# Node sums by three small products, pair 1's marks behind the first layer, and a quad's weights in one iteration

## The chip, the cores and the metric

The kernel runs on one core of one Trainium2 chip. A core has a matrix engine (TensorE, called PE in the profile, with its weight loads shown apart as PEld), a vector engine (VectorE, DVE), a scalar engine (ScalarE, ACT), a general engine (GpSimd, POOL) and a sequencer that issues most DMAs (SyncE, SP). They run side by side, each through its own instructions in the order in which these were written, and wait for each other through semaphores. The metric is the device time of one execution in microseconds (us), over several runs. The profiled execution has a time of its own and a span, from its first to its last instruction.

## The reference, cut to what matters

A graph layer over 128 graphs of 64 nodes with 128 features. Every pair of nodes (i, j) gets a message from a three-layer perceptron; the messages are masked by the adjacency `adj[b, i, j]` (0 or 1, about an eighth of it set, the diagonal always) and summed over j; a second perceptron updates the node.

```python
pair_feats = concat([f_i, f_j], axis=-1)
h = layernorm(relu(pair_feats @ w0 + b0))
h = layernorm(relu(h @ w1 + b1))
messages = (h @ w2 + b2) * adj[..., None]
agg = sum(messages, axis=2)
out = x + mlp_upd(concat([x, agg], axis=-1))
```

Messages where `adj` is 0 count for nothing, so only the edges that are set need computing. The layer norms have gain one and shift zero here, but the kernel takes them as they come.

## The kernel before, in words

**Edges as slots.** Each graph gets 640 slots, one per edge, packed in order of node; the slots are five tiles of 128. Two graphs make a *pair* (64 of them, both graphs side by side on the 128 partitions), two pairs a *quad* (32), four pairs a *block* (16). Slots are worked on in *chunks* of 512 columns: five chunks a quad, ten a block, 160 in all. A flag at the end of the kernel sends graphs with more than 640 edges, or weights other than 0 and 1, through a second, dense path; with these inputs it isn't taken.

**Finding the slots of a block.** `rank` (DVE, L354) makes running sums of the adjacency along each row, so its last column is each node's degree. `count` (PE, L363) multiplies the degrees by the triangular matrix `lt` (one triangle for each graph of a pair): that gives the sums of degrees up to and with each node, `cumall`. `count_out` and `degrees` copy both to SBUF on ACT. `place` (POOL, L374) takes the degrees off `cumall` (`before`: the sum of the nodes ahead), adds the two (`mid`: twice the middle of the node's range of slots), and adds `before` to the ranks (`pos`). `place_out` masks `pos` by the adjacency into `posall`, and `odd_marks` and `odd_weights` prepare the check for weights other than 0 and 1.

**Gather lists of a pair.** A slot belongs to a node if its distance from `mid` is less than the degree: `distance` (ACT, L467) and `make_tp` (DVE, L473) make `tp`, a 0/1 matrix of nodes by slots. `node_rows` (ACT, L479) casts it, and `stack` (SP, L486) copies it by DMA into the upper half of `S[p]`. `marks` (PE, L495) multiplies `posall` by `tp`, and `compare` (DVE, L503) compares the outcome with the slot's number, which gives a 0/1 matrix of the second nodes; another `stack` puts it into the lower half of `S[p]`. Pair 0 is done ahead of the loop, without DMA: its compares write `S[0]` at once. Pair 1 has its marks, compares and stacks ahead of the loop too.

**The chunk pipeline.** `layer0` (PE, L521) multiplies the projected features of both nodes (`abl` and `abh`, a low and a high part, made from `xnT` by `rows`, `rows_hi` and `rows_lo`) by the slots of `S`, and ACT evicts it with relu as `h`. `stats0` turns `h` on PE (L530) and DVE takes its statistics. Eight iterations later `layer1` (PE: a bias product at L567, then L570) goes into the one bank `z`, ACT evicts it as `y` (L573), and `stats1` takes its statistics. At a quad's end `var0_of` (POOL, L247 to L251) makes `m`, `root_of` takes the root on ACT (`m_sd`), casts its high part on ACT (`sh`, L548) and makes the low part on POOL (`sh`, L549), and `turn_root` (PE, L554) turns it for the bias product. `var1_step`, `root1_of` and `inverse_of` give the second norm's factors `m_q`. `node_marks` turns `tp` by a DMA into `oh`, `weights` (POOL, L636; DVE for the last quad) multiplies `oh` by the factors for each of the two graphs of a pair, and `reduce` (PE, L651) sums `y` by node.

**Updates.** Each block has a `Unit` (the last block two) that runs the second perceptron: `sums_out`, `turn`, `layer` (PE, L696 and L710), `layer_out` (DVE), the roots with POOL's `um_v` and ACT's `um_sq`, the biases `m0` and the residual `xo` on POOL, and `finish`.

**The order of the work.** It is written out by hand. `at(n, place, fn)` puts a step into iteration `n` of the main loop at a named place; the loop runs the places in the order a, m, layer 1, b, layer 0, stats0, k, stats1, x, x1, x2, e0, e1, e. So each engine's queue is the order in which these steps are called. `L1` is 8 iterations, a quad has `QC` = 5. The steps for the turned root of a quad q stand in iteration 5q + 6; before the change the weights of quad q's even pair stand in iteration 5q + 15 and those of its odd pair in 5q + 16, in place e1. Behind the weights come the residual and the bias of a unit, then `place` of a later block, all in place e. Buffers that matter: one PSUM bank each for `mk`, `hps`, `hT` and `z`; four `S`; two each of `d`, `i`, `j` and `w`.

**The start.** Loads are issued on SP in the order in which they are first used, the first layer's two weight matrices on ACT. Seven products of a constant run on PE while they land. `place_first` (DVE, L395) makes `before` and `mid` of block 0, and `place_pair` (DVE, L407) the masked positions of one pair of it.

Of the kernel before, what the change touches and what calls it, by code (L numbers as in the profile page):

```python
# [23 lines left out]
def tile_gnn(  # L24
# [68 lines left out]
    def mat(ap, name, eng=nc.sync):  # L93
        return load(ap, [P, C], name, eng)
# [11 lines left out]
    def load_first(b, q0, q1):  # L106
        nc.sync.dma_start(xn0[:, b, q0:q1], xf[(b * PB + q0) * P:(b * PB + q1) * P, :]
                          .rearrange("(q p) c -> p q c", p=P))

    nc.sync.dma_start(an0[:, 0], adjp[:, 0:PB, :])  # L110
    load_first(0, 0, 2)
    w0a = mat(mw0[0:C, :], "w0a", nc.scalar)
    w0b = mat(mw0[C:2 * C, :], "w0b", nc.scalar)
# [29 lines left out]
    lt = const.tile([P, P], F32, name="lt")  # L143
    nc.gpsimd.memset(lt, 1.0)
    nc.gpsimd.affine_select(out=lt, in_=lt, pattern=[[1, P]], compare_op=ALU.is_ge,
                            fill=0.0, base=0, channel_multiplier=-1)
    nc.gpsimd.memset(lt[0:N, N:P], 0.0)
# [4 lines left out]
    make_identity(nc, ident)  # L152

# [12 lines left out]
    cumall = const.tile([P, NP], F32, name="cumall")  # L166
# [120 lines left out]
    def edge_path(es):  # L287
# [72 lines left out]
        def count(b):  # L360
            blk = blocks[b]
            blk["ps"] = abank()
            nc.tensor.matmul(blk["ps"][:, 0:PB], lhsT=lt, rhs=blk["rk"][:, :, N - 1], start=True,  # L363
                             stop=True)

        def count_out(b):
            nc.scalar.copy(cumall[:, b * PB:(b + 1) * PB], blocks[b].pop("ps")[:, 0:PB])
# [6 lines left out]
        def place(b):  # L374

            blk = blocks[b]
            cum = cumall[:, b * PB:(b + 1) * PB]
            before = adp.tile([P, PB], F32, name="before")
            nc.gpsimd.tensor_tensor(before, cum, blk["deg"], op=ALU.subtract)
            blk["mid"] = adp.tile([P, PB], F32, name="mid")  # L380
            nc.gpsimd.tensor_tensor(blk["mid"], cum, before, op=ALU.add)  # L381
            pos = adp.tile([P, PB, N], F32, name="pos")
            nc.gpsimd.tensor_tensor(pos, blk.pop("rk"),
                                    before.unsqueeze(2).to_broadcast([P, PB, N]), op=ALU.add)
            blk["pos"] = pos
# [9 lines left out]
        def place_first():  # L395
            blk = blocks[0]
            rk = blk["rk"]
            before = blk["before"] = adp.tile([P, PB], F32, name="before")
            nc.vector.tensor_tensor(before, cumall[:, 0:PB], rk[:, :, N - 1], op=ALU.subtract)
            blk["mid"] = adp.tile([P, PB], F32, name="mid")  # L400
            nc.vector.tensor_tensor(blk["mid"], cumall[:, 0:PB], before, op=ALU.add)

        def place_pair(q):
            blk = blocks[0]
            for g in range(2):
                s = slice(g * N, (g + 1) * N)
                nc.vector.scalar_tensor_tensor(posall[s, 0, q, g, :], blk["rk"][s, q],  # L407
                                               blk["before"][s, q:q + 1], blk["an"][s, q],
                                               op0=ALU.add, op1=ALU.mult)
# [54 lines left out]
        def distance(p):  # L464
            b, q = divmod(p, PB)
            D[p] = tpp.tile([P, CAP], F16, name="d", bufs=2)
            nc.scalar.activation(D[p], slot, AF.Abs, bias=blocks[b]["mid"][:, q:q + 1], scale=-1.0)  # L467
# [347 lines left out]
        for p in range(NP):  # L815
            n = p * TG * 2 // CH
            if p > 1:
                at(max(n - 7, p - 2), "a", distance, p)
                at(max(n - 6, p - 2), "m", make_tp, p)
                at(max(n - 5, 1), "a", node_rows, p)  # L820
                at(max(n - 4, 1), "a", stack, p, 0, IR)
                for k in range(2):
                    at(n - 5 + k, "k", marks, p, k)
                    at(n - 5 + k, "k", compare, p, k)
                at(n - 3, "a", stack, p, 1, JR)
            w = p // 2 * QC + QC + L1 + p % 2
            last = p // 2 == NQ - 1
            at(w - 4, "a", node_marks, p)
            at(NCHK + L1 + 1 if last else w + 2, "e1", weights, p)
            at(NCHK + L1 + 2 if last else p // 2 * QC + SC, "x1", reduce, p)  # L830
# [19 lines left out]
        rank(0)  # L850
        count(0)
        count_out(0)
        turn_x(0, 0, 2)
        turn_x_out(0, 0, 2)
        degrees(0)
        place_first()
# [4 lines left out]
        rows_hi(0, 0)  # L861
# [4 lines left out]
        for g in range(2):  # L866
            s = slice(g * N, (g + 1) * N)
            nc.scalar.copy(S[0][0:N, g, :], TP[0][s])
# [4 lines left out]
            if g == 0:  # L873
                rows_lo(0, 0)
                distance(1)
        MK.pop((0, 0)), MK.pop((0, 1))
        place_pair(1)
        make_tp(1)
        node_rows(1)
        stack(1, 0, IR)  # L880
        for k in range(2):
            marks(1, k)
            compare(1, k)
        stack(1, 1, JR)
        nc.vector.memset(ones_row, 1.0)
        at(0, "x", turn_x, 0, 2, PB)
        at(0, "a", lambda: place_pair(2))
        at(1, "m", lambda: place_pair(3))
        at(1, "a", lambda: turn_x_out_rest())
        at(1, "e", odd_marks, 0)  # L890
# [230 lines left out]
```

## Time and profile before

| | us |
|---|---|
| median of three runs | 614.89 (614.76 to 615.21) |
| the profiled execution | 615.34 |
| its span | 613.6 |
| PE busy | 577.3 |
| DVE busy | 478.1 |
| ACT busy | 379.1 |
| POOL busy | 361.7 |
| one block of the steady part, start to start | 35.04 |

A line of the timeline has the start and the duration in us, the engine and line, the operation with the tiles that it writes and reads, the shape, the number of instructions that are merged in it, and in brackets how long the engine had been idle and what ended that. PE's ends are modelled, so distances between starts are the safer figures. A line of the list of waits has who waited for whom, the total in us, how many times, and the longest. One PE product in full precision shows as two passes (x2), a transpose as one.

### The profile page before, as it was taken

Reading aid. Unit: us, or ns where it says so; the run is one execution under the profiler, and the core shown is the slowest. Engines: PE = TensorE matmul, PEld = TensorE weight load, DVE = VectorE, ACT = ScalarE, POOL = GpSimd, SP = SyncE. Lnnn points to the kernel's source line nnn. Section 1 sums busy time; section 2 is a strip of 40 time slices with the busy share of each in tenths; the row PEclk is TensorE's granted clock in tenths of the full one; section 3 lists DMA queues with packets and bytes.
Section 4 is the critical chain, followed back from the end, with each engine's and each line's share of the span. In section 5 each row is a group of like instructions: output and inputs, shape, how many; then the busy total and the mean of one; then the engine's idle time right before and its main releaser. Section 6 shows DMA issues by size and latency. Waiting matters only on the chain. (4 is left out here: it accounts for less than half of the span.)

```text
span 613.6 us, 15457 instructions
## 1 busy us (share of the span) xinstructions
PE 577.3 (94%) x5393; PEld 532.1 (87%) x5393; DVE 478.1 (78%) x1868; ACT 379.1 (62%) x781; POOL 361.7 (59%) x919
## 2 busy tenths in 40 slices
PE   5888999999999999999999999999999999998875
PEld 4677889998999999898999999899999989898763
DVE  5767668897878889787878889787888978776574
ACT  4676666676667567576656667666656657653412
POOL 2634375675838476574839567583847657463742
PEclk9999999999999999999999999999999999999987
DMA  4654455545354663734464554535544444331101
GB/s 100 155 126 116 105 114 115 93 118 114 86 144 117 121 116 103 117 89 118 118 132 107 130 96 114 117 85 142 118 121 106 108 114 97 86 84 41 24 18 37
DMA packets 91085, 63.84 MB, mean 104 GB/s; under 512 B 57462, under 2 KB 74876, under 8 KB 91004
## 3 DMA queue, kind: packets, MB, share of 16 engines
q1 hardware_dynamic: 90716, 62.69, 45.1%
q8 instruction: 44, 0.72, 0.5%
q14 instruction: 37, 0.30, 0.2%
q10 hardware_dynamic: 288, 0.13, 0.1%
HBM read 6.82 MB, written 4.19 MB: 18 GB/s over the span
## 5 line engine op out<-in xcount | busy, mean ns | idle before, releaser
L534 DVE BATCH_NORM_STATS2 st<-hT 128x6 f32<-128x128 f32 x640 | 141.9, 284 | 49.0 <-PE hT L530 47.3
L570 PEld LDWEIGHTS z<-w1c,h 128*128 128x128 f32 x1280 | 168.3, 192 | 6.9
L570 PE MATMUL z<-w1c,h 128*128 128x128 f32 x1280 | 168.8, 275 | 0.0
L580 DVE BATCH_NORM_STATS2 st<-y 128x6 f32<-128x128 f32 x640 | 137.7, 277 | 14.7 <-ACT y L573 14.6
L573 ACT ACTIVATE y<-z 128x512 f32<-128x512 f32 x160 | 95.2, 595 | 77.4 <-PE z L570 77.4
L524 ACT ACTIVATE h<-hps,b0c 128x512 f32<-128x512 f32 x160 | 109.3, 683 | 2.3 <-PE hps L521 2.2
L247 POOL TENSOR_TENSOR m_d<-st 128x20 f32<-128x20 f32 x62 | 15.5, 250 | 146.7 <-DVE st L534 131.1
L530 PE MATMUL hT<-ident,h 128*128 128x128 f32 x640 | 97.2, 275 | 0.0
L636 POOL TENSOR_TENSOR w<-oh,m_q 128x320 f32<-128x320 f16 x124 | 91.8, 761 | 5.8 <-PE hT L530 5.0
L521 PE MATMUL hps<-s,abl 128*128 128x512 f32 (+3 forms) x256 | 92.1, 372 | 0.4 <-ACT h L524 0.4
L530 PEld LDWEIGHTS hT<-ident,h 128*128 128x128 f32 x640 | 76.3, 141 | 9.9 <-DVE st L534 0.3
L567 PE MATMUL z<-b1t,sdT 80*128 80x512 f32 x160 | 78.4, 490 | 1.6 <-ACT y L573 1.6
L521 PE MATMUL hps<-s,abh 128*128 128x512 f32 (+3 forms) x256 | 78.3, 324 | 0.0
L651 PE MATMUL ys<-y,w 128*64 128x128 f32 x1280 | 77.1, 275 | 0.0
L651 PEld LDWEIGHTS ys<-y,w 128*64 128x64 f32 x1280 | 69.3, 137 | 7.3 <-issue 7.0
L467 ACT ACTIVATE d<-slot,mid 128x640 f16<-128x640 f16 x64 | 53.3, 833 | 34.2 <-POOL mid L381 34.2
L503 DVE TENSOR_TENSOR j<-mk,cmpt 128x320 fp32r<-128x320 f32 x126 | 59.6, 473 | 1.6 <-PE mk L495 1.6
L458 DVE TENSOR_TENSOR abl<-mu,abh 128x512 fp32r<-128x512 f32 x32 | 22.1, 691 | 39.9 <-ACT abh L451 39.9
L521 PEld LDWEIGHTS hps<-s,abl 128*128 128x128 f32 x256 | 49.5, 193 | 1.8 <-ACT i L479 0.9
L479 ACT CAST i<-tp 128x640 fp32r<-128x640 f16 x63 | 45.5, 722 | 7.5 <-DVE tp L473 7.4
L521 PEld LDWEIGHTS hps<-s,abh 128*128 128x128 f32 x256 | 49.5, 193 | 0.0
L451 ACT CAST abh<-mu 128x512 fp32r<-128x512 f32 x32 | 18.8, 587 | 45.8 <-PE mu L444 45.8
(221 smaller groups left out, 1017.3 us busy)
## 6 DMA issues: line engine op xcount, KB each, us to landing
s<-i SPq DMA_DIRECT2D x126, 160.0 KB, 2.7
s<-j SPq DMA_DIRECT2D x126, 160.0 KB, 2.6
xn<-in_x_dram SPq DMA_DIRECT2D x15, 256.0 KB, 3.9
out_dram<-uo SPq DMA_DIRECT2D x15, 256.0 KB, 2.4
an<-in_adj_dram SPq DMA_DIRECT2D x16, 128.0 KB, 2.7
oh<-tp SPq DMA_TRANSPOSE x64, 2.7
xn<-in_x_dram SPq DMA_DIRECT2D x2, 128.0 KB
out_dram<-uo SPq DMA_DIRECT2D x2, 128.0 KB
```

The costliest lines, as they stand in the source:

```text
L467: nc.scalar.activation(D[p], slot, AF.Abs, bias=blocks[b]["mid"][:, q:q + 1], scale=-1.0)
L503: nc.vector.tensor_tensor(JR[p][:, c], MK.pop((p, k))[:, 0:HC], cmpt[:, c], op=ALU.is_equal)
L521: nc.tensor.matmul(ps[:, c:c + w], lhsT=ab[:, g % 4, :], rhs=s, start=(k == 0), stop=(k == 1))
L524: nc.scalar.activation(H[n], ps, AF.Relu, bias=b0c)
L530: nc.tensor.transpose(ps[:, t, :], H[n][:, t * P:(t + 1) * P], ident)
L534: nc.vector.bn_stats(ST0[q][:, CH * c + t, :], ps[:, t, :])
L567: nc.tensor.matmul(ps, lhsT=SD[q], rhs=W["b1t"][:, CH * c:CH * c + CH, :], start=True, stop=False, skip_group_check=True)
L570: nc.tensor.matmul(ps[:, t, :], lhsT=h[:, t * P:(t + 1) * P], rhs=W["w1c"], start=False, stop=True, skip_group_check=True)
L573: nc.scalar.activation(Y[n], ps, AF.Relu)
L580: nc.vector.bn_stats(ST1[q][:, CH * c + t, :], Y[n][:, t, :])
L636: (nc.vector if p // 2 == NQ - 1 else nc.gpsimd).tensor_tensor(w[:, :, g, :], OH[p][:, :, g * N:(g + 1) * N], Q[q][:, k:k + TG].unsqueeze( ...
L651: nc.tensor.matmul(YS[b][g * N:(g + 1) * N, k, :], lhsT=w[:, t, g, :], rhs=y, start=(t == 0), stop=(t == TG - 1))
```

## The change

Four edits to the order of the work, and one to how the sums are made.

1. *Sums.* `lt` becomes three matrices: the triangle, the triangle without its diagonal, and their sum. `count` multiplies the degrees by all three, so that PE gives `cumall`, `before` (as `befall`) and `mid` (as `midall`), and `count_out` copies all three at once. `place` keeps only `pos`; `place_first` is gone; `distance` reads `midall`, so it waits for ACT's own copy only.
2. *Loads.* The first two pairs' features are loaded through ACT's queue, the first layer's two weight matrices through SP's.
3. *The first block.* The features are turned ahead of the count. Pair 0's node rows come ahead of `rows_hi`, pair 1's place and `tp` ahead of the second graph's compares. Pair 1's marks, compares, node rows and stacks move into iteration 0 of the loop, behind layer 0 of chunk 0. `place_pair` of pairs 2 and 3, `odd_marks(0)` move to later places.
4. *Pairs 2 and 3.* `distance` and `make_tp` a step later or the same, marks and compares and the second stack one iteration later, the first stack at p + 1.
5. *Weights.* Both pairs of a quad have their weights in iteration 5q + 16, behind `sh` of the quad that is turned there.

```diff
-    load_first(0, 0, 2)
-    w0a = mat(mw0[0:C, :], "w0a", nc.scalar)
-    w0b = mat(mw0[C:2 * C, :], "w0b", nc.scalar)
+    load_first(0, 0, 2, nc.scalar)
+    w0a = mat(mw0[0:C, :], "w0a")
+    w0b = mat(mw0[C:2 * C, :], "w0b")
...
+    nc.gpsimd.tensor_tensor(lt[:, 1], lt[:, 0], ident, op=ALU.subtract)
+    nc.gpsimd.tensor_tensor(lt[:, 2], lt[:, 0], lt[:, 1], op=ALU.add)
...
-    cumall = const.tile([P, NP], F32, name="cumall")
+    cums = const.tile([P, 3, NP], F32, name="cums")
+    cumall, befall, midall = (cums[:, k] for k in range(3))
...
-            nc.tensor.matmul(blk["ps"][:, 0:PB], lhsT=lt, rhs=blk["rk"][:, :, N - 1], start=True,
-                             stop=True)
+            for k in range(3):
+                nc.tensor.matmul(blk["ps"][:, k * PB:(k + 1) * PB], lhsT=lt[:, k],
+                                 rhs=blk["rk"][:, :, N - 1], start=True, stop=True)
...
-            nc.scalar.copy(cumall[:, b * PB:(b + 1) * PB], blocks[b].pop("ps")[:, 0:PB])
+            nc.scalar.copy(cums[:, :, b * PB:(b + 1) * PB],
+                           blocks[b].pop("ps")[:, 0:3 * PB].rearrange("p (k q) -> p k q", k=3))
...
-            cum = cumall[:, b * PB:(b + 1) * PB]
-            before = adp.tile([P, PB], F32, name="before")
-            nc.gpsimd.tensor_tensor(before, cum, blk["deg"], op=ALU.subtract)
-            blk["mid"] = adp.tile([P, PB], F32, name="mid")
-            nc.gpsimd.tensor_tensor(blk["mid"], cum, before, op=ALU.add)
             pos = adp.tile([P, PB, N], F32, name="pos")
             nc.gpsimd.tensor_tensor(pos, blk.pop("rk"),
-                                    before.unsqueeze(2).to_broadcast([P, PB, N]), op=ALU.add)
+                                    befall[:, b * PB:(b + 1) * PB].unsqueeze(2).to_broadcast([P, PB, N]),
+                                    op=ALU.add)
...
-            nc.scalar.activation(D[p], slot, AF.Abs, bias=blocks[b]["mid"][:, q:q + 1], scale=-1.0)
+            nc.scalar.activation(D[p], slot, AF.Abs, bias=midall[:, p:p + 1], scale=-1.0)
...
-                at(max(n - 7, p - 2), "a", distance, p)
-                at(max(n - 6, p - 2), "m", make_tp, p)
-                at(max(n - 5, 1), "a", node_rows, p)
-                at(max(n - 4, 1), "a", stack, p, 0, IR)
+                early = p < PB
+                at(p - 1 if early else n - 7, "a", distance, p)
+                at(p - 1 if early else n - 6, "m", make_tp, p)
+                at(p if early else n - 5, "a", node_rows, p)
+                at(p + 1 if early else n - 4, "a", stack, p, 0, IR)
                 for k in range(2):
-                    at(n - 5 + k, "k", marks, p, k)
-                    at(n - 5 + k, "k", compare, p, k)
-                at(n - 3, "a", stack, p, 1, JR)
+                    at(n - 5 + early + k, "k", marks, p, k)
+                    at(n - 5 + early + k, "k", compare, p, k)
+                at(n - 3 + early, "a", stack, p, 1, JR)
...
-            at(NCHK + L1 + 1 if last else w + 2, "e1", weights, p)
+            at(NCHK + L1 + 1 if last else p // 2 * QC + QC + L1 + 3, "e1", weights, p)
...
+        turn_x(0, 0, 2)
         count(0)
+        degrees(0)
+        turn_x_out(0, 0, 2)
         count_out(0)
-        turn_x(0, 0, 2)
-        turn_x_out(0, 0, 2)
-        degrees(0)
-        place_first()
         distance(0)
         place_pair(0)
         make_tp(0)
         rows(0, 0)
-        rows_hi(0, 0)
...
+        node_first(0)
+        rows_hi(0, 0)
+        compare_first(0)
+        rows_lo(0, 0)
+        distance(1)
+        node_first(1)
         place_pair(1)
         make_tp(1)
-        node_rows(1)
-        stack(1, 0, IR)
+        compare_first(1)
+        MK.pop((0, 0)), MK.pop((0, 1))
         for k in range(2):
-            marks(1, k)
-            compare(1, k)
-        stack(1, 1, JR)
+            at(0, "k", marks, 1, k)
+            at(0, "k", compare, 1, k)
+        at(0, "b", node_rows, 1)
+        at(0, "e", stack, 1, 0, IR)
+        at(0, "e", stack, 1, 1, JR)
         nc.vector.memset(ones_row, 1.0)
         at(0, "x", turn_x, 0, 2, PB)
-        at(0, "a", lambda: place_pair(2))
-        at(1, "m", lambda: place_pair(3))
+        at(0, "e", place_pair, 2)
+        at(1, "e", place_pair, 3)
         at(1, "a", lambda: turn_x_out_rest())
-        at(1, "e", odd_marks, 0)
+        at(6, "e", odd_marks, 0)
```

`node_first(g)` and `compare_first(g)` are the node rows and the two compares of pair 0's graph g, as they stood in the loop before.

## The prediction, made before the changed kernel was run

> **What bounds the kernel now.** I began with the page's busy shares and its 40 slices: TensorE (PE) is busy for 94% of the span and at "9" from slice 5 to slice 37, so the kernel is bound by PE's order of work, except in the first 30 us and the last 50 us.
>
> ```profile
> PE 577.3 (94%) x5393; PEld 532.1 (87%) x5393; DVE 478.1 (78%) x1868; ACT 379.1 (62%) x781; POOL 361.7 (59%) x919
> ...
> PE   5888999999999999999999999999999999998875
> ```
>
> Next the list of who waits for whom, for PE's few waits. The largest is on `sh`, the last step of a quad's standard deviations on GpSimd (POOL); the second is in the first block. ScalarE (ACT) waits a lot for `mid`, but ACT isn't the bound.
>
> ```profile
> PE ma L554 <- POOL sh L549: 10.6, 18, 1.9
> ...
> PE mk L495 <- DVE tp L473: 4.6, 2, 3.4
> ...
> ACT d L467 <- POOL mid L381: 34.2, 13, 2.7
> ```
>
> Then the timeline of one steady block (two quads, 35.04 us start to start, the same for twelve blocks). PE's lines around the node count and around the two turned roots (L554):
>
> ```profile
> 303.19 0.60 PE L696 MATMUL ma<-ident,ysum 128*128 128x128 f32 x4
> 303.54 0.48 PE L567 MATMUL z<-b1t,sdT 80*128 80x512 f32 x1
> ...
> 307.69 0.27 PE L554 MATMUL ma<-ident,sh 128*80 128x128 f32 x1
> ...
> 310.86 0.60 PE L428 MATMUL ma<-ident,xn 128*128 128x128 f32 x4
> 311.30 0.28 PE L363 MATMUL ma<-rk,lt 128*128 128x4 f32 x2
> 311.44 0.48 PE L567 MATMUL z<-b1t,sdT 80*128 80x512 f32 x1
> ...
> 324.14 1.05 PE L710 MATMUL mu<-u1c,uhT 128*128 128x128 f32 x8
> 325.57 0.31 PE L554 MATMUL ma<-ident,sh 128*80 128x128 f32 x1 [0.38 <-POOL sh L549]
> ```
>
> One root of a block comes without a wait, the other waits. POOL shows why: two weight products stand between `m` and `sh`, although ACT's half of `sh` was cast by 324.53.
>
> ```profile
> 323.52 0.41 POOL L251 TENSOR_TENSOR m<-m_d,m_s 128x20 f32<-128x20 f32 x1
> 323.89 1.40 POOL L636 TENSOR_TENSOR w<-oh,m_q 128x320 f32<-128x320 f16 x2
> 325.25 0.27 POOL L549 TENSOR_TENSOR sh<-m_sd,sh 128x40 fp32r<-128x40 f32 x1
> 325.48 1.40 POOL L636 TENSOR_TENSOR w<-oh,m_q 128x320 f32<-128x320 f16 x2
> 326.83 1.29 POOL L690 TENSOR_TENSOR xo<-xn,cu2b 128x512 f32<-128x512 f32 x1
> ```
>
> [...] weight loads around L363 start 0.11 us apart, for 4 moving columns as for 128. [...] passes are 0.21 us apart until 19.6 us and 0.11 after it. [...]
>
> **The change, part by part.** All times are of the profiled execution (span 613.6, 615.34 us in all).
>
> *1. Three count products in place of one.* One is two passes with 128 weight columns. With it the four transposes at 310.86 lead to L567 after 0.58 us; without it the same four (303.19) lead to L567 after 0.35. So one product costs 0.23, two more about 0.45 us per block. PE has no wait from there to 325.57, and that wait is on POOL's work on statistics that come after the count on PE, so nothing absorbs it. Blocks 2 to 15 pay it at full clock: 14 x 0.45 = **+6.3**. (Blocks 0 and 1 are in part 5.) ACT's copy of 12 columns instead of 4 stays 0.17 us, in ACT's free time.
>
> *2. Weights after `sh`.* In a steady block POOL then waits for ACT's cast (324.53), runs `sh` at 324.61 to 324.88 (the 0.08 us from cast to `sh` as at 45.60/45.68), and PE can turn at 324.93. PE itself is free at 325.03 (L710's eight passes, 0.11 each), against 325.57: -0.54. But POOL now idles from 323.93 to 324.61, so its four weights end later: `xo` starts at 324.61 + 0.225 + 4 x 0.68 = 327.56 instead of 326.83, +0.73. Removing `before` and `mid` (330.44 to 330.87) gives back 0.43, so `um_v` comes 0.29 later. ACT waits for `um_v`, and `y`, which frees PE's bank, stands behind it:
>
> ```profile
> 333.16 0.30 ACT L271 ACTIVATE um_sq<-um_v,eps_c 128x4 f32<-128x4 f32 x1 [0.32 <-POOL um_v L265]
> 333.37 0.57 ACT L677 COPY ysum<-ys 128x512 f32<-128x512 f32 x1
> 333.83 0.59 ACT L451 CAST abh<-mu 128x512 fp32r<-128x512 f32 x1
> 334.87 0.60 ACT L573 ACTIVATE y<-z 128x512 f32<-128x512 f32 x1 [0.44 <-PE z L570]
> ```
>
> ACT could take `y` 0.5 us after `abh` starts, at 334.33; it will be 334.62. PE's `z`, moved 0.54 ahead, is ready for it at 334.33. So `y` is 0.29 late, and PE's next L567, which today follows `y` by 0.05 us, loses that. Behind `abh` on DVE, `abl`, `tp` and the statistics move by the same 0.29 and hold the next transposes another 0.08. Left: -0.54 + 0.29 + 0.08 = -0.17, for twelve blocks (115.32 to 500.77): **-2.0**. At 535.59 no later block is placed, which spares POOL a further 0.6 us (`pos`): the gain stays, **-0.5**. Of the early roots, 81.61 gains 0.63 (81.61 to 80.98; no update unit's roots yet in that block); 63.66 would gain 0.63, but `cu2b_b`'s copy ends at 63.40 and holds the next product: 0.37. Together **-1.0**. 31.81 and 46.00 have no weights before them: 0. Reduction stands two iterations behind the weights and keeps over 1 us. In the block's other quad POOL waits 2.06 us for DVE after the weights, which covers the later end.
>
> *3. The end.* For quad 29 POOL runs the first weights at 566.75, in idle time. Afterwards all four stand behind `sh` (569.56), so `xo`, `m` and `um_v` are 2 x 0.68 later, and ACT already waits for `um_v` with `ysum` and `y` queued behind:
>
> ```profile
> 576.46 0.30 ACT L271 ACTIVATE um_sq<-um_v,eps_c 128x4 f32<-128x4 f32 x1 [2.43 <-POOL um_v L265]
> ...
> 577.78 0.51 PE L567 MATMUL z<-b1t,sdT 80*128 80x512 f32 x1 [0.72 <-ACT y L573]
> ```
>
> PE's wait at 577.78 grows by the whole of it, and what follows is a chain: **+1.4**.
>
> *4. Sums without POOL and DVE.* ACT's `d` no longer waits for `mid` (34.2 us in all). In these stretches PE is reducing and never waits for ACT's next `y`: 0. `odd_marks(0)` moves to iteration 6, behind `sh` on POOL, with the bias table's last three parts 1.34 us later behind it; these end at 34.75 now, and their next user is layer 1's second chunk at 38.09: 0, from 2 us of cover.
>
> *5. The first block.* Pair 0: the transposes go ahead, at about 4.3 (the warm products end there); three products at half clock take 6 x 0.21, so the sums are copied at 6.2 instead of 5.5, but two DVE steps fall out and `d` starts at 6.4 as now. The rows start at 6.1 instead of 6.48, the marks at 8.0 instead of 8.39. DVE then needs two compares, `abl`, place, `tp`, two compares, the ranking and one compare (0.41 + 0.49 + 0.70 + 0.61 + 0.35 + 0.90 + 0.70 + 0.49), and the first two layer-0 products go ahead of pair 1's marks (10.2 instead of 13.57). PE's unbroken run starts with pair 1's second marks at 13.2 instead of 16.06, but holds one more mark product and two more counts: 1 us more at half clock, so layer 0 of chunk 2 starts at 17.8 instead of 19.60. On SP, one weight load more and the adjacency load go ahead of pair 1's gathers: these are issued at 13.4 to 15.8 and, at the 2.5 to 2.7 us that such gathers take, land by 18.0, just ahead of the 18.3 at which chunk 2 needs them. Behind it ACT has pair 2's cast and pair 3's distance ahead of `h` of chunk 2 (about 19.1 instead of 20.60). What reaches the steady part: **-1.5**. Pair 2's gathers (by 24.5) are ready for chunk 5 (25.2).
>
> Sum: 6.3 - 2.0 - 0.5 - 1.0 + 1.4 - 1.5 = **+2.7 us**, 618.0 for the profiled execution, which lies 0.45 above the median of 614.89: I predict **617.5**.
>
> **Rivals.** (a) *No giving back*: against PE's new time `um_v` comes 0.83 us later (0.29 + 0.54), and `y` has a slack of 0.54 today (334.33 to 334.87). If a shorter run of POOL work[...] keeps the shift under 0.54, nothing is held and the twelve blocks keep 0.54: 12 x 0.37 = 4.4 us less, 613.1, faster than before by over 0.2%. It decides once less than 0.05 of the 0.37 is lost per block. For it: POOL's weights took 1.40 in this quad and 1.78 in the other, so its times do move. Against: POOL runs from 326.83 to 338.0 without a pause that could take up the shift. Chance 0.10. (b) *The weight loads of the small products hide*: a product costs half of 0.23, 614.4; from nothing (611.2) to the whole lie the bounds. Against it is the measured 0.23. 0.08. (c) *The clock comes late*: after its run from 13.2 PE pauses near 19 us; [...] iterations 3 and 4 run at half clock, some 1.2 us: 618.7. 0.12. (d) *The first block gains more*: [...] `h` of chunk 2 isn't held; up to 3 us there, 616. 0.10. (e) My forecast, 616 to 619: 0.60.
>
> **How the numbers follow.** A measurement here can tell about 0.2%, 1.2 us, from no change: 613.7 to 616.1. Faster: (a) and a third of (b), 0.13. Same: the rest of (b), part of (d) and the forecast's lower edge, 0.16. Slower: 0.71. The range 613.6 to 619.4 leaves out most of (a) and the far end of (c); the slower cases alone have 616.2 to 619.4.
>
> **What would show it.** Right: the block period rises from 35.04 to about 35.3; L363's line has six passes and L567 follows the transposes by 1.03; L554 shows no wait from 98 us on, but L567 waits some 0.3 for `y` ten us later; the wait at 577.78 is near 2 us; layer 0 of chunk 2 starts near 17.8. Wrong: a period under 35.04, `y` without a wait behind `um_sq`, or a first block that is over 2.5 us ahead at 32 us.

## The result and the profile after

The changed kernel took 624.78 us (median of 4 runs, 622.57 to 625.70) against 615.05 us for the kernel before: a ratio of 1.0142, with a 95% interval of 1.0101 to 1.0183. The sign was forecast, the size was not: 617.5 us was predicted, with a range up to 619.4. The profiled execution took 625.70 us, the slowest of the four; its span is 624.0 us.

The first view of the page: engines, and the 40 slices of TensorE (PE) and of the clock it was granted (9 is full). The last line is the clock's row of the kernel before.

```profile
PE 592.2 (95%) x5457; PEld 543.7 (87%) x5457; DVE 463.1 (74%) x1866; ACT 379.2 (61%) x781; POOL 353.7 (57%) x891
...
PE   7888999999999999999999999999999999998874
...
PEclk9789999999999999999999999999999999999887
...
PEclk9999999999999999999999999999999999999987
```

PE is busier than before (592 against 577 us), with 64 records more: two more products of two passes in each of 16 blocks. The row of the clock differs: in the second and third slice, between 15.6 and 46.8 us, it isn't full, though PE was at work long before. (The row counts the time ahead of the clock's first record as full. In both kernels PE began at half clock: passes start 0.21 us apart there, and 0.11 later. The first record of a full clock is at 20.14 us before and at 16.51 after.)

The waits (total, times, longest):

```profile
PE ma L547 <- POOL sh L542: 4.5, 5, 1.9
PE z L560 <- ACT y L566: 3.2, 4, 2.1
PE mu L209 <- ACT b1b_b L208: 1.5, 1, 1.5
...
ACT um_sq L275 <- POOL um_v L269: 51.1, 15, 3.8
```

The wait for `sh` fell from 10.6 us to 4.5 (18 times to 5), as forecast. ACT's wait for `mid` (34.2 us) is gone, and its wait for `um_v` rose from 9.0 to 51.1. New on PE are a wait of 2.1 us for `y`, at the end, and one of 1.5 us in the first block.

A steady block answers the forecast line by line. First the count, then the root, GpSimd's (POOL's) weights behind `sh`, and ACT's queue ahead of the `y` in dispute:

```profile
316.21 0.60 PE L422 MATMUL ma<-ident,xn 128*128 128x128 f32 x4
316.64 0.73 PE L368 MATMUL ma<-rk,lt 128*128 128x4 f32 x6
317.23 0.48 PE L560 MATMUL z<-b1t,sdT 80*128 80x512 f32 x1
...
330.81 0.27 PE L547 MATMUL ma<-ident,sh 128*80 128x128 f32 x1
```

```profile
330.39 0.27 POOL L542 TENSOR_TENSOR sh<-m_sd,sh 128x40 fp32r<-128x40 f32 x1 [0.68 <-ACT sh L541]
330.61 2.76 POOL L629 TENSOR_TENSOR w<-oh,m_q 128x320 f32<-128x320 f16 x4
```

```profile
339.22 0.30 ACT L275 ACTIVATE um_sq<-um_v,eps_c 128x4 f32<-128x4 f32 x1 [3.58 <-POOL um_v L269]
339.42 0.57 ACT L670 COPY ysum<-ys 128x512 f32<-128x512 f32 x1
339.89 0.59 ACT L445 CAST abh<-mu 128x512 fp32r<-128x512 f32 x1
340.37 0.61 ACT L566 ACTIVATE y<-z 128x512 f32<-128x512 f32 x1
```

From the transposes to L560 it is 1.02 us (forecast 1.03), the turned root has no wait, and `y` stands behind `um_sq`, `ysum` and `abh`, which came with `um_v`. PE's next L560 came at 341.03, 0.06 us after `y`'s end.

Setting each chunk's first h transpose against the same one in the profile before gives the sum, term by term:

| term | forecast | in the profile |
|---|---|---|
| first block (up to chunk 10, less one count) | -1.5 | +3.5 |
| two more count products, 14 times | +6.3 | +6.3 (0.45 each) |
| weights behind `sh` | -3.5 | -3.2 |
| from the last transposes to the end | +1.4 | +3.8 |
| sum | +2.7 | +10.4 |

The steady period went from 35.04 to 35.37 us (the mean of eleven blocks; about 35.3 was forecast): in a block the step at the root is -0.57, ten us later +0.39 and +0.05, at the count +0.45. The terms that are well off are the first block, by 5.0 us, and the end, by 2.4.

**The end.** The forecast wait is there, and the row that answers to 577.78 of before is

```profile
585.73 0.50 PE L560 MATMUL z<-b1t,sdT 80*128 80x512 f32 x1 [2.10 <-ACT y L566]
```

which is +1.37. But the next two layers take 3.16 and 3.41 us where they took 2.09 and 2.94, +1.54. The view of busy times by stretch, cut every 3.41 us, since the ten records of the granted clock in this profile begin that or a multiple of it apart (the columns: stretch, its length, busy us and instructions of PE, weight loads, VectorE (DVE), ACT and POOL, then the granted clock, DMA share and GB/s), shows why:

```profile
583.12:586.54 3.42, 1.32 (x11) 1.08 (x10) 1.01 (x5) 1.50 (x4) 2.57 (x13) 1.00 0.00 0
586.54:589.95 3.41, 3.41 (x18) 3.31 (x17) 1.19 (x6) 1.85 (x4) 2.76 (x4) 0.50 0.00 0
589.95:593.36 3.41, 3.41 (x31) 3.37 (x31) 1.55 (x5) 0.60 (x1) 0.00 (x0) 1.00 0.00 0
```

The wait made a stretch of 3.41 us in which PE worked 1.32, and for the next 3.41 us the clock was half. The rest, 0.9 us, lies behind the last products, mostly in the last transfer and the closing steps; from the last transposition to the end the profiles of this study have 5.8 to 7.1 us, whatever the kernel.

**The first block.** The same view from 16.51 us, where the clock first became full:

```profile
16.51:19.93 3.42, 2.15 (x18) 1.79 (x16) 3.37 (x9) 2.45 (x7) 2.26 (x4) 1.00 0.39 91
19.93:23.34 3.41, 3.22 (x12) 2.80 (x13) 1.28 (x6) 2.08 (x4) 2.00 (x6) 0.50 0.49 122
23.34:26.75 3.41, 3.41 (x21) 2.44 (x20) 1.55 (x7) 1.02 (x3) 1.76 (x4) 0.50 0.71 165
26.75:30.17 3.42, 2.67 (x16) 1.57 (x14) 3.25 (x9) 2.70 (x5) 1.40 (x2) 1.00 0.00 0
30.17:33.58 3.41, 1.42 (x10) 1.07 (x9) 3.41 (x13) 1.45 (x5) 2.48 (x7) 1.00 0.78 192
33.58:36.99 3.41, 3.19 (x15) 3.09 (x16) 0.63 (x4) 2.09 (x6) 3.33 (x5) 0.50 0.60 153
```

Twice the clock fell back to half, behind stretches in which PE waited and worked 2.15 and 1.42 us. In the profile of before it never did from 20.14 us up to 593 us. PE's wait for the first root was as long there (1.86 us), but the border of two stretches (30.38 us, counted on from 20.14 in steps of 3.41) cut it into stretches with 2.63 and 1.98 us of work, and the clock stayed full:

```profile
26.97:30.38 3.41, 2.63 (x18) 1.76 (x16) 2.85 (x12) 1.67 (x4) 2.69 (x7) 1.00 0.72 169
30.38:33.79 3.41, 1.98 (x18) 1.97 (x19) 1.76 (x9) 2.94 (x8) 3.41 (x6) 1.00 0.29 72
```

So the second loss isn't the new order's own: two kernels below with the old order (`e2_counts` and `e5_weights_dve`) have it in their profiles too (half clock from 32.22 and from 34.10 us), and one whose first block is that of the changed kernel (`e12_after_oldend`) doesn't.

The changed order itself came as forecast up to there: chunk 2's layer 0 at 17.25 us (forecast 17.8), the transposes of chunks 0 and 1 ahead by 2.5 us. The wait that came next was not in the forecast. PE's product of the second derived matrix, then DVE's and POOL's work around it:

```profile
20.12 0.77 PE L209 MATMUL mu<-w,b1b_b 128*128 128x128 f32 x2 [1.46 <-ACT b1b_b L208]
```

```profile
14.41 0.57 DVE L401 SCALAR_TENSOR_TENSOR posall<-rk,cums,an 64x64 f16<-64x64 f32 x2
15.01 0.39 DVE L466 TENSOR_SCALAR tp<-d,deg 128x640 f16<-128x640 f16 x1
...
17.55 1.40 DVE L401 SCALAR_TENSOR_TENSOR posall<-rk,cums,an 64x64 f16<-64x64 f32 x2
18.98 0.85 DVE L466 TENSOR_SCALAR tp<-d,deg 128x640 f16<-128x640 f16 x1
19.75 0.27 DVE L189 TENSOR_TENSOR w1c<-w1c_g,mu 128x128 f32<-128x128 f32 x1
```

```profile
17.45 0.61 POOL L384 TENSOR_TENSOR pos<-rk,cums 128x256 f32<-128x256 f32 x1 [13.57 <-ACT cums L372]
18.14 1.50 POOL L394 TENSOR_TENSOR posall<-pos,an 64x256 f16<-64x256 f32 x2
```

The wait is put down to ACT, but `b1b_b` was there at 19.58; what came last was `w1c` on DVE (19.75 to 20.02), which empties the bank. It stood behind `place_pair(2)`, whose two steps took 1.40 us where those of pair 1 (14.41) took 0.57, and a `make_tp` of 0.85 where that of pair 1 (15.01) took 0.39, while POOL placed block 1. That PE waited from 18.67 made the stretch up to 19.93 a thin one.

### The profile page after: what moved, and what is told of

Read it like the earlier page. It is cut to its first block, busy times and chain, and to the rows that moved or that the text cites. A ratio compares the mean times of both kernels' runs of the same rounds, so it can differ in the third digit from the quotient of the medians.

```text
span 624.0 us, 15556 instructions
## 1 busy us (share of the span) xinstructions
PE 592.2 (95%) x5457; PEld 543.7 (87%) x5457; DVE 463.1 (74%) x1866; ACT 379.2 (61%) x781; POOL 353.7 (57%) x891
## 4 chain that ended last, share of the span: by engine, by line
## 5 line engine op out<-in xcount | busy, mean ns | idle before, releaser
L523 PE MATMUL hT<-ident,h 128*128 128x128 f32 x640 | 98.9, 278 | 0.3 <-DVE st L527 0.3
L629 POOL TENSOR_TENSOR w<-oh,m_q 128x320 f32<-128x320 f16 x124 | 85.6, 720 | 0.9 <-issue 0.8
L560 PE MATMUL z<-b1t,sdT 80*128 80x512 f32 x160 | 78.5, 491 | 4.2 <-ACT y L566 3.2
L460 ACT ACTIVATE d<-slot,cums 128x640 f16<-128x640 f16 x64 | 53.1, 829 | 0.1
```

Source lines behind the costliest of these rows:

```text
L460: nc.scalar.activation(D[p], slot, AF.Abs, bias=midall[:, p:p + 1], scale=-1.0)
L523: nc.tensor.transpose(ps[:, t, :], H[n][:, t * P:(t + 1) * P], ident)
L560: nc.tensor.matmul(ps, lhsT=SD[q], rhs=W["b1t"][:, CH * c:CH * c + CH, :], start=True, stop=False, skip_group_check=True)
L629: (nc.vector if p // 2 == NQ - 1 else nc.gpsimd).tensor_tensor(w[:, :, g, :], OH[p][:, :, g * N:(g + 1) * N], Q[q][:, k:k + TG].unsqueeze( ...
```

## The experiments

**One part each.** `e1_weights`, `e2_counts` and `e3_first` put one part into the kernel before, `e4_after_fill` leaves the change whole and gives PE idle work.

```
e1  -  at(NCHK + L1 + 1 if last else w + 2, "e1", weights, p)
    +  at(NCHK + L1 + 1 if last else p // 2 * QC + QC + L1 + 3, "e1", weights, p)
e2  -  nc.tensor.matmul(blk["ps"][:, 0:PB], lhsT=lt, rhs=blk["rk"][:, :, N - 1], ...)
    +  for k in range(3 if b else 1):
    +      nc.tensor.matmul(blk["ps"][:, k * PB:(k + 1) * PB], lhsT=lt[:, k], ...)
       and no before and mid of blocks 1 to 15 on POOL
e3     the changed kernel, with
    +  for k in range(1 if b else 3):            # count
    +  nc.gpsimd.tensor_tensor(befall[:, s], cumall[:, s], blk["deg"], op=ALU.subtract)
    +  nc.gpsimd.tensor_tensor(midall[:, s], cumall[:, s], befall[:, s], op=ALU.add)
       and the weights' times of before
e4     the changed kernel, with
    +  at(2, "x", fill, 6)          # idle products mean_m x mean_m, in a bank of their own
    +  if q == 0: fill(8, SD[q])    # in turn_root
```

> The kernel before with one edit: a quad's two weight products on GpSimd both come behind sh. In the trace of the changed kernel its share of the steady blocks reads as the -0.57 us at each block's turned root, less +0.33 us given back half a block later (0.39 + 0.05, less what the count adds nothing to). My theory (the gain at the root is nearly all given back through um_v, um_sq and y): blocks 2 to 15 end 3 to 3.5 us earlier, the end costs +1.4 us, and +1.5 us more if the clock falls in the longer wait for y: 613 to 615 us. Rival (nothing is given back; the held y came from the count products): 12 x 0.57 + 1.6 = 8.4 us earlier before the end, 608 to 610 us.

> The kernel before with one edit: blocks 1 to 15 take their node sums from three count products instead of one, block 0 and the order of the first block stay. My theory: 14 x 0.45 + 0.5 = +6.5 to +6.8 us, 621.5 to 622 us, each block 0.45 us longer at the count and nothing given back. Rival (the small products' weight loads hide in part, or the two GpSimd steps that fall out bring the next root forward): under 619 us.

> The kernel before with one edit: the first block's new order alone, with three count products in block 0 only; the later blocks' sums and weights as before. Theory (the order gains some 1 us, and TensorE, ahead of the others, then waits so long inside one of the clock's windows that the clock is halved twice): 618 to 620 us, with windows at half clock after 20 us in the profile. Rival (the new order loses by itself, since GpSimd's and VectorE's products now fall together): also slower[...]. If neither holds and it is as forecast: 613.5 us.

> The changed kernel with idle products of constants in TensorE's queue at the two waits of the first block (6 ahead of the second derived matrix, 8 ahead of the first turned root), which leave every other engine's work as it is. If the halved clock makes the loss: no half-clock window between 20 and 37 us, and 4 to 5 us less than the changed kernel, 619.5 to 621 us. If the waits themselves or the order make it: no gain, or 1 us slower from the idle products, 624 to 626 us.

| run | median us (runs) | ratio to before, interval | steady period | chunk 10 against the profile before |
|---|---|---|---|---|
| e1_weights | 618.19 (20) | 1.0050, 1.0035 to 1.0066 | 35.32 | -1.7 |
| e2_counts | 624.44 (4) | 1.0160, 1.0108 to 1.0211 | 35.45 | +2.2 |
| e3_first | 616.44 (20) | 1.0021, 1.0006 to 1.0035 | 35.02 | +2.3 |
| e4_after_fill | 622.22 (4) | 1.0120, 1.0067 to 1.0173 | 35.36 | +0.3 |

The weights alone make the kernel slower by 0.5%, which no one of my expectations said: they win 0.57 at the root and lose 0.16, 0.64 and 0.05 in the iterations after. ACT's queue in that profile, and the waits:

```profile
330.66 0.83 ACT L467 ACTIVATE d<-slot,mid 128x640 f16<-128x640 f16 x1 [4.01 <-POOL mid L381]
331.40 0.58 ACT L573 ACTIVATE y<-z 128x512 f32<-128x512 f32 x1
```

```profile
PE z L567 <- ACT y L573: 7.2, 15, 2.1
```

`d` waits for POOL's `mid`, and `y` behind `d`; `um_v` too has the 0.43 us of `before` and `mid` ahead of it, which the changed kernel doesn't have on POOL. The counts alone cost 0.45 us at each count and give back nothing but 0.04. In the median of four runs that range from 622.74 to 627.36 they come out 9.3 us slower than before, more than I expected (6.5 to 6.8); the profile is 7.4 slower, and loses some 1.6 us of it with the clock at the first root. The steady blocks of the parts add up to +0.28 + 0.41 = +0.69 a block, the change has +0.33: the two parts aren't independent, since the count products take from POOL what the weights' new place needs there.

The first block's order alone costs 0.2% in the median, where I had forecast a gain; its profile, the second slowest of 20 runs, shows half clock from 8.38 to 25.44 us and from 32.27 to 35.68. With idle products the changed kernel has no half-clock stretch from 21.34 to 598 us in its profile, and chunk 10 comes at 44.90 instead of 48.55. But the medians are 0.2 points apart with overlapping intervals, and the first rise of the clock differs from profile to profile, so this alone didn't settle it; `e4` missed its range by 1.2 us. The clock's stretches begin at another time after the start in each profile (20.14 us before, 16.51 after, 4.92 in `e2_counts`, whose first block is that of before but for the count products of blocks 1 and 2), and with the same code in the first block chunk 10 comes at other times: -1.7 in `e1_weights`, whose first block is that of before, and +2.4 instead of +3.9 in `e12_after_oldend`, whose first block is that of the changed kernel.

**What gives the gain back.** `e5` and `e9` take `before` and `mid` off POOL's path ahead of `um_v` without more count products, `e6` takes the residual product off it.

```
e5  weights as e1, and in place():
    -  nc.gpsimd.tensor_tensor(before, cum, blk["deg"], op=ALU.subtract)
    +  nc.vector.tensor_tensor(before, cum, blk["deg"], op=ALU.subtract)     # mid too
e9  weights as e1, and before and mid of place() in a function of their own:
    +  at(max(o - 10, r + 1), "e0", sums, b)
       at(max(o - 9, r + 1), "e", place, b)
e6  -  at(n + t[8], "e", residual, u)
       at(n + t[9], "e", upd_m1, u)
    +  at(n + t[9], "e", residual, u)           # the last two blocks as before
    +  at(... p // 2 * QC + QC + L1 + 3 - (p // 2 > NQ - 4 and p % 2 == 0), "e1", weights, p)
```

> The kernel before with the two weight products behind sh (as in e1_weights), and with the two small sums before and mid of a block on VectorE instead of GpSimd; TensorE keeps its one count product. Theory (in e1_weights ACT's d waited for mid, y stood behind d, and so the block lost 0.16 + 0.64 + 0.05 where it won 0.57; what the changed kernel's three products gave back was GpSimd's 0.43 us): the period falls from 35.32 of e1_weights to 34.9, -0.13 against before; 12 x 0.41 = 5 us less than e1_weights, 613 us. Rival (the third iteration's loss comes from the weights themselves, which hold um_v whatever follows): period 35.3 as in e1_weights, 618 us.

> e1_weights again, with before and mid taken off the path in another way than in e5: they stay on GpSimd, but ahead of the quad's statistics, where GpSimd idles for 7 us, in place of 2 us ahead of um_v. Theory (those 0.43 us ahead of d and um_v decide whether the weights' place gains or loses): the period goes from 35.32 to 34.9 (0.57 won, 0.44 lost), some 5 us under e1_weights, 613 us. Rival (the place of the weights loses by itself): 35.3.

> The kernel before with the two weight products behind sh except for the last three quads, and GpSimd's 1.29 us residual product (xo) behind um_v instead of ahead of it, except for the last two blocks. If um_v is what gives the gain back: nothing is lost in a block after the root, the period is 35.04 - 0.57 = 34.47, and the end costs nothing: 12 x 0.57 + 0.34 + 0.63 + 0.57 = 8.4 us less than before, 606.5 to 607 us. Rival (another engine takes over once the root is early, for example y through ACT's own queue): period 34.9 or more, 612 us or more.

| run | median us (runs) | ratio to before, interval | steady period |
|---|---|---|---|
| e5_weights_dve | 625.08 (4) | 1.0175, 1.0148 to 1.0202 | 35.50 |
| e9_weights_sums | 613.70 (10) | 0.9988, 0.9972 to 1.0004 | 34.90 |
| e6_weights_resid | 609.26 (6) | 0.9919, 0.9894 to 0.9945 | 34.63 |

`e5` missed, for a reason that tells nothing of the question: PE lost 1.0 us in another iteration, waiting for DVE (12 times, 10.0 us). The two sums of four columns took 0.68 and 0.65 us there, against 0.15 to 0.16 in blocks 1 and 2, where POOL was idle as they began. Each ends just behind one of POOL's weight products (0.69 us apiece):

```profile
330.72 2.08 POOL L636 TENSOR_TENSOR w<-oh,m_q 128x320 f32<-128x320 f16 x3
...
331.47 0.68 DVE L379 TENSOR_TENSOR before<-cumall,deg 128x4 f32<-128x4 f32 x1
332.18 0.65 DVE L381 TENSOR_TENSOR mid<-cumall,before 128x4 f32<-128x4 f32 x1
```

`e9` put the question without this: 34.90, with -0.57, +0.38 and +0.05 per block. So POOL's 0.43 us decide whether the weights' place gains or loses, and in the change it is the count products that take them away. In `e6` the 0.39 is gone too, and ACT's wait for `um_v` with it, which is 50.8 us in the profile of `e9`:

```profile
ACT um_sq L271 <- POOL um_v L265: 7.7, 15, 1.8
```

Some 0.15 us is lost an iteration later, and the block is 0.41 us shorter than before, not the 0.57 that I expected; the median missed its range by 2.3 us. That `um_v` gives the 0.39 back is shown; what holds the 0.15 is not.

**The clock.** Idle products in every long wait of PE in the first block, in the order of before (`e10`) and in the new one (`e11`, `e13`), and in the whole change (`e14`); `e7` has them at two waits only.

```
fill(n): n products mean_m x mean_m, in a bank of their own
e7   e3 with fill 6 and 8 at the places of e4
e10  before with fill(12) ahead of marks(1, 0), fill(2) ahead of marks(1, 1), fill(4) ahead of
     marks(2, 0), fill(8) in turn_root(0)
e11  e3 with fill(5) ahead of layer0(0), fill(5) ahead of marks(1, 1), fill(5) ahead of the
     second derived matrix, fill(8) in turn_root(0)
e13  e11 without the third
e14  the changed kernel with the three of e13
```

> The first block's new order alone (as e3_first), with idle products in TensorE's queue at its two long waits. If the halved clock is what the new order costs: no half-clock window after 20 us in the profile, and 1.5 to 3 us less than e3_first in the median, 613.5 to 615 us, level with before or just under it. If VectorE's and GpSimd's crowded work makes the loss: as e3_first, 616.4 us.

> The kernel before with idle products in every long wait of TensorE in the first block (12, 2, 4, and 8 ahead of the turned root), so that the clock is full from some 7 us on in every run. Theory (the start of the run against the clock's windows decides the time of the first block): a narrow spread, the first block 1.5 to 2.5 us ahead of the profile of before, 613 us. Rival (the first block is bound by the others): 615 us and the spread of before.

> The first block's new order alone (e3_first) with idle products in every long wait of TensorE there (5, 5, 5, and 8). If the forecast of the new order was right but for the clock: 1 to 1.5 us less than e10_before_hold, 611.5 to 612 us. If the new order loses or gains nothing even at full clock, since GpSimd's and VectorE's work falls together in it: e10_before_hold or more, 613 to 614 us.

> e11_first_hold without the 5 idle products ahead of the second derived matrix, which there held that product back from some 18.9 us to 19.41. Theory (at full clock the new order's lead of 1 us at chunk 0 is spent waiting for pair 1's gathered rows, which land no earlier): 0.5 us under e11 in the first block, so 0.3 us ahead of e10_before_hold, not the 1.5 us of the forecast; the time is 613 to 614 us. Rival (the order is worth its 1.5 us): 1.5 us ahead of e10_before_hold at the end of the first block.

> The changed kernel with idle products in TensorE's waits of the first block (5, 5 and 8). With the clock out of the first block, the forecast's other terms should stand alone against e10_before_hold: blocks 1 to 15 +2.7, the end +1.4 (up to 3 with a half-clock window in the longer wait), the order -0.3: 3.8 to 5.5 us over e10_before_hold, 617 to 618.5 us. Rival (the changed kernel loses more in its first block for another reason than the clock): 621 us or more.

| run | median us (runs) | ratio to before, interval | chunk 0, 1, 2 and 10 against the profile before |
|---|---|---|---|
| e7_first_fill | 615.92 (8) | 1.0022, 1.0001 to 1.0043 | -2.5, -2.6, -1.9, -1.9 |
| e10_before_hold | 613.06 (20) | 0.9979, 0.9966 to 0.9992 | -2.3, -2.5, -2.5, -2.5 |
| e11_first_hold | 614.93 (20) | 1.0008, 0.9995 to 1.0021 | -3.4, -2.7, -2.2, -2.2 |
| e13_first_hold2 | 614.90 (12) | 0.9995, 0.9979 to 1.0011 | -3.5, -2.6, -2.4, -1.0 |
| e14_after_hold | 621.95 (4) | 1.0100, 1.0076 to 1.0123 | -3.4, -2.7, -2.5, +0.3 |

`e10` shows that the clock is worth time in the old order itself: nothing but idle work was added, its profile has full clock from 4.96 to 592 us, and it is 0.2% faster. Not every run of `e10` is as fast: three of the 20 took some 615.3 us. `e7` is no faster than `e3_first` by the intervals. Yet its profile, with full clock from 16.87 to 556 us, has chunk 10 1.9 us ahead of the profile before, where the clock rises at 20.14: with a clock that rises early and then holds, the forecast's -1.5 against that profile does come out. Whether the clock held in the other seven runs isn't known.

`e11` and `e13` show what the new order is worth once PE is at full clock early. Against `e10` it is 1 us ahead at chunk 0, 0.2 at chunk 1, and the lead is spent at chunk 2. PE in `e11_first_hold`, then DVE's compares of pair 1 in `e10_before_hold` and in `e11_first_hold`:

```profile
17.42 0.35 PE L518 MATMUL hps<-s,abl 128*128 128x256 f32 x1 [1.05 <-DMA s<-j]
```

```profile
11.60 0.49 DVE L503 TENSOR_TENSOR j<-mk,cmpt 128x320 fp32r<-128x320 f32 x1 [0.41 <-PE mk L495]
12.48 0.49 DVE L503 TENSOR_TENSOR j<-mk,cmpt 128x320 fp32r<-128x320 f32 x1 [0.39 <-PE mk L495]
```

```profile
12.94 0.49 DVE L500 TENSOR_TENSOR j<-mk,cmpt 128x320 fp32r<-128x320 f32 x1
13.82 0.49 DVE L500 TENSOR_TENSOR j<-mk,cmpt 128x320 fp32r<-128x320 f32 x1 [0.39 <-PE mk L492]
```

The new order brings pair 0 forward and puts pair 1 back by 1.3 us, and its gathered rows land at 17.4 us, 1.05 to 1.2 us after PE is there. In `e13` that wait made the next thin stretch:

```profile
16.68:20.09 3.41, 2.24 (x13) 1.72 (x14) 2.59 (x8) 2.66 (x5) 3.12 (x6) 1.00 0.54 129
20.09:23.50 3.41, 3.41 (x25) 2.87 (x23) 1.38 (x6) 1.14 (x4) 1.54 (x6) 0.50 0.61 145
```

and cost 1.4 us between chunk 2 and chunk 3. So with full clock in both, the new order equals the old one within 0.3 us by the profiles (`e11`: -2.2, though idle products delayed one product there by some 0.5; `e10`: -2.5): at equal clock the order gains nothing. The median of `e11` is 1.9 us above that of `e10`, and above the ranges of both its expectations. Its profile lost 1.5 us at another place: behind PE's wait of 1.89 us ahead of the product of the flag (it ends at 555.08 us) the clock is half from 555.55 to 558.96. Six of the 16 profiles have that loss, the one of before not; its share in the medians isn't measured. `e14` came out some 3.5 us above the end of what I expected, as high as its rival said: its first block has the same half-clock stretch (20.14 to 23.55) and, not by the clock, 0.8 us more at the statistics of chunk 4, behind a `make_tp` that took 1.24 us beside a step of POOL and 0.38 in `e13`; its end has the half-clock stretch behind the wait for `y`.

**The end.** `e12` moves the weights of the last three quads back in the changed kernel (of the last quad they have a time of their own in both).

> The changed kernel, with the weights of the last three quads back at their place of before. Theory (the four weights behind sh make um_v, um_sq and y 1.4 us late, and the longer wait can halve the clock for one window more): 1.4 to 2.9 us less than the changed kernel, 621.9 to 623.4 us, with the wait ahead of the last but one y at 0.7 us instead of 2.1. Rival (the end is bound by the update of the last block, and the wait is made up for): 624.5 us.

620.32 us (4 runs), ratio 1.0091, 1.0057 to 1.0125: 1.6 us under the range that I expected. The row at the wait:

```profile
582.83 0.50 PE L560 MATMUL z<-b1t,sdT 80*128 80x512 f32 x1 [0.75 <-ACT y L566]
```

The part from the last transposes to the end takes 48.2 us, against 51.6 in the changed kernel and 47.8 before: the 1.37 us of the wait and the 1.54 of the clock are both gone. A further 1.5 us of the difference between the two profiles lies in the first block, which has the same code in both. The same wait is in the profiles of `e1`, `e4`, `e5` and `e9` (+1.34 to +1.38 us) without a half-clock stretch behind it, and in `e14` with one: the wait is in all six profiles with the new place of the weights at the end, the half-clock stretch behind it in two. What decides that isn't shown.

**A version that beats both.** `e8_best` is `e6` with idle products at three waits of the first block (7, 4 and 8) and at two of the end (8 and 4, ahead of the turned `uy` of the last block's halves).

> e6_weights_resid with idle products at four waits of the first block (7 ahead of pair 1's marks, 4 ahead of pair 2's, 8 ahead of the first turned root) and of the last (8 and 4 ahead of the turned uy of its two halves); the order of the first block is that of before, the count is one product. Theory (each half-clock window costs up to 1.7 us where TensorE is the bound): 1.5 to 3 us less than e6_weights_resid, 604 to 605.5 us, and a narrower spread. Rival (the waits there are bound by other engines whatever the clock): as e6_weights_resid.

607.99 us (4 runs, 607.52 to 609.02), ratio 0.9903, 0.9874 to 0.9931: faster than both kernels, but 2.5 us over the range that I expected. The range of its runs is 1.5 us, against 3.4 of `e6` (6 runs), and the medians are 1.3 apart, with overlapping intervals. If the idle products gained that, it was in the first block (chunk 10 is 0.7 us earlier than in `e6`, from profiles that differ in the clock's stretches): at the end they cost 1.1 us, 25.7 us from the last layer 1 to the last transposition, where the other profiles have 24.4 to 24.6.

## Why the prediction was wrong, by its own steps

*Step 1, three counts.* Right: 0.45 us each, on PE's path, and nothing absorbs it (`e2_counts`).

*Step 2, weights behind `sh`.* Right in mechanism and size: -0.13 per block against -0.17, -3.2 against -3.5 in all. The step took the 0.43 us of `before` and `mid` off in the same sum; `e1` and `e9` show that without this the sign turns. Rival (a), no giving back, fell: 0.39 is held in every block, because `um_v` comes late. So did rival (b), hidden weight loads, by the 0.45 of step 1.

*Step 3, the end.* The wait was right (+1.37 for +1.4); it lacked the half clock behind it, +1.54 in this profile.

*Step 4, sums without POOL.* I costed ACT's `d` at nothing because nothing waits for it today. With the weights moved, something does: in `e1` PE's `y` stood behind it. Within the whole change it is still nothing.

*Step 5, the first block: this is the step that failed*, in its last sentence, "What reaches the steady part: -1.5". Its times were right up to chunk 2 (17.25 us for 17.8). Behind it I let the lead run on at full clock, and didn't ask what PE would wait for next when it is early. It waited 1.46 us for DVE's `w1c`, behind steps that took 1.40 and 0.85 us beside POOL's work where those of pair 1 took 0.57 and 0.39, and the clock went back to half; then it waited for the first root, as in the old order, and the clock fell again. In `e7`, whose profile loses no clock there, the same order is 1.9 us ahead. I had also written that pair 1's rows would land "just ahead" of their need; once the clock is full early they land 1 us late, and against an old order with the same clock nothing is left of the lead. The step's sum came out at +3.5 us in the profile, and the order alone at 0.2% slower (0.06 to 0.35%) in 20 runs: rival (d), a larger gain in the first block, went the other way.

*Rival (c), the clock comes late*, was the right resource with the wrong event and price. I took the clock for a thing that PE earns once, at 1.2 us if late; that was my estimate, and no trace had shown it. (I read its rise before at 19.6 us, off the passes; the clock's record has 20.14.) In the changed kernel it rose early (16.51 us), was lost twice in the first block and once more behind the wait for `y`. The profiled execution missed 618.0 by 7.7 us: 5.0 in the first block, 1.5 in the half clock behind `y`, 0.9 at the closing and 0.3 in step 2. How the 5.0 divide between the lead that didn't last and the two losses isn't measured.

What stays open: which busy share of a stretch keeps the clock. In the profiles of before and of the changed kernel, from the first record of a full clock on, the full-clock stretches with 1.76 us of PE or more kept it, but for the one with 2.15, and the five with 1.71 or less lost it. But `e3_first` lost it behind 2.10 and behind 1.77 us, and `e13` behind 2.24: no one share divides these records. The 2.15 hold six count passes of 4 columns, which start 0.11 us apart like those of 128. Nor is the share of the clock in the median's loss measured, since each profile is one start against its stretches. By the medians the order alone is 1.3 us slower than before, where a gain of 1.5 was forecast: 2.8 of the 7.3 us by which the median was missed. The counts alone came out at 9.3 us there for 6.5 to 6.8 expected, with an interval that begins at 1.1%, 6.6 us. So the split by steps above is that of one execution.

## What to carry to other kernels

A path that gets one engine ahead is worth only what the next wait on that engine leaves: follow it to the first point where it meets another engine's old pace. Where that engine is TensorE, the new wait can cost twice: at the end of this kernel +1.37 us of wait, then +1.54 at half clock. The new waits with half clock behind them were of 1.20 (`e13`), 1.46 and 2.10 us (the changed kernel); a forecast has to ask for waits of that size whether the work behind them will run at half clock. One profile then shows one start of the kernel against the clock's stretches; small differences take many runs. Two edits that share an engine's queue are costed together: here one of them lost alone and gained beside the other.

## What the runs showed of the hardware

In the profiles of before and of the changed kernel, and in the first 36 us of `e3_first`, all changes of the clock lie 3.41 us or a multiple apart. They don't stand at a fixed time after the kernel's start: with the same order of the first block the clock first falls to half at 8.38 us in `e3_first` and at 19.93 in the changed kernel, 11.55 apart, which is no multiple. Stretches of 3.41 us with 1.32, 1.42 and 2.15 us of PE's work (the changed kernel) and 2.24 (`e13`) were followed by half clock. The 47 runs of the kernel before beside `e9` to `e12` lie between 613.0 and 618.1 us in groups: 14 below 613.7, 19 from 614.1 to 615.1, 11 from 615.8 to 616.5, three from 617.8. What makes the groups isn't shown, since only one run of this kernel has a trace. Where waits were filled (`e10`), half of the 20 runs lie within 0.4 us.

DVE's two sums of four columns (`e5`) took 0.65 to 0.69 us each in all 13 blocks in which POOL was at work, as long as the POOL step beside them (0.69) and ending with it, and 0.15 to 0.16 where POOL was idle. What makes them longer isn't shown.
